# Seven products instead of eight in two more places of a four-layer graph network, with GpSimd taking the element-wise steps around them

## The chip, the cores and the metric

The kernel is one program on one core of a Trainium2 chip. The core has a matrix engine (TensorE, in the profile PE, its weight loads PEld), a vector engine (VectorE, DVE), a scalar engine for activation functions (ScalarE, ACT), a general engine (GpSimd, POOL) and an engine that here only issues transfers (SyncE, SP). Each works through a queue of its own in order, and semaphores tie the queues together. Matmuls read SBUF and write PSUM, which is divided into banks of 128 x 512 float32. The metric is the time of one execution in device microseconds. Before the change three runs took 2252.04, 2249.4 and 2255.14 us (median 2252.04).

## The reference

The input x is (128, 64, 256) in float32: 128 graphs of 64 nodes with 256 features. Four layers follow, each of the form x = x + f(relu(layernorm(x))). Two of them matter here, both in the third layer:

```python
h = relu(einsum('ts,bsh->bth', adj, x @ Wg0 + bg0))
h = relu(einsum('ts,bsh->bth', adj, h @ Wg1 + bg1))
for p in range(1, 5):                       # MAX_SKIP = 4
    nw = Tv // p                            # Tv = 64 nodes
    wins = h[:, :nw * p, :].reshape(Bv * nw, p, Hd)
    last = lstm_last(Wih[p - 1], Whh[p - 1], bih[p - 1], bhh[p - 1], wins)
    h = h.at[:, arange(nw) * p + (p - 1), :].set(last)
```

That is two graph convolutions and then four LSTMs, one for each window length p. The LSTM of a window runs p steps from a zero state with c = sigmoid(f) * c + sigmoid(i) * tanh(g) and h = sigmoid(o) * tanh(c), and its last h replaces the window's last node. With p = 1 a window is one node: one step, no recurrent product, no forget gate, and every one of the 64 nodes is replaced.

## The kernel before

**Layout.** The 8192 rows (128 graphs x 64 nodes) are 16 blocks of 512. X0 to X15 are sixteen SBUF tiles of 128 x 1024 float32, one a block. In the third layer the features are the partitions: `big` is four tiles (groups of four blocks), seen by `nodes` (L1767) as 2 feature halves x 64 nodes x 32 graphs.

**Order.** PE, DVE and ACT instructions go through a recording helper, `Ordered.__getattr__.call` (L788, its call is L799), so in the profile all of them carry L799 and tiles tell them apart. GpSimd instructions carry their own lines. Inside a stage a tile scheduler puts the instructions into each engine's queue; there is no hand-written order in the two stages of the change. A tile that is taken again makes its next writer wait for its readers.

**Third layer, graph convolutions** (`layer2`, L2147; a step is `block`, L2174). For block i: the first weight, `ps<-a,w`, two PSUM tiles of 128 x 512 with two matmuls each, then a maximum with a table N0 on DVE into `g`; `features` of block i-1 (`ps<-BDA,y`, the adjacency product, relu on ACT into `big`); `mixed` of block i+1 (`ps<-BDA,h`, its two halves evacuated into `a`, one by DVE and one by ACT, in turn through `move`, L1487); the second weight, `pt<-w,g`, with the sum into `y` on DVE; and the layer norm of block i+2, whose X tile is then written to DRAM (`xs<-X`, L2156), since the LSTMs use the X tiles as scratch. There are 4 `ps` banks, 2 `pt` banks and 2 `pe` banks.

**LSTMs** (`windows`, L2204; `lstm`, L2294). For each p the nodes are cut into chunks of up to 16 windows of one group; a chunk is 256 columns at p = 1, 16 chunks in all, taken in pairs. `gates` (L2321) forms the pre-activations of one or two gates. A weight of 256 x 256 is split into four 128 x 128 quarters and the operand into four parts of 128 x W columns, and seven products of such quarters and their sums (`product`, L2337, in the order 1, 6, 7, 5, 2, 4, 3) replace eight. The partial sums live in four banks a, b, f and d of a ring of seven `ps` banks. Product 1 is copied to Z (`ls_z`) on ACT, and DVE adds: Z += product 6; U = Z + product 7; one quarter = U + product 5; then Z plus bank f (after product 4) and Z plus bank d (after product 3). ACT applies sigmoid or tanh to the four quarters. The sums of the operand's parts are three DVE subtractions into `ls_tx` (one of 128 x 512, two of 128 x 256), those of the weights four DVE instructions a weight.

At p = 1 the input and cell gates (0, 2) of one chunk go together by seven products. The output gate (3) goes alone: four matmuls of 512 columns into two banks, with two activations. DVE multiplies i and g (`X<-ls_g`, 128 x 1024), ACT takes the tanh, and `last_state` (L2396) multiplies on DVE in two instructions of 128 x 512 into `big`.

**Weights.** `load` (L2224) and `weights` (L2232) place the LSTM weights: those for odd p in X tiles (Whh in X0 to X3, Wih in X4 to X7), those for even p in tiles of their own; the DMAs are on SP (L2239). The weights for p + 1 are asked for after the first pair of p's chunks. X8 to X15 are rings for c, h, U and others.

## Time and profile before

| quantity | value |
|---|---|
| median of three runs | 2252.04 us |
| the profiled execution's own time | 2254.63 us |
| its span | 2252.8 us |
| mean granted clock of TensorE | 0.997 |
| busy: PE, DVE, ACT, POOL | 2214.0, 1610.7, 1143.7, 7.2 us |
| POOL instructions | 33 |
| p = 1: first PE instruction, first of p = 2 | 677.64, 830.53 us |
| PE idle at the start of p = 1 | 0.85 us |
| DVE busy from 500 to 550, 600 to 650 us (of 50) | 43.6, 19.7 us |

The profile is of one execution, and all sums below are made against that execution. A busy share is an average over stages: only some 167 us of third-layer blocks (16 of 10.46 us, PE rows from 593.81 to 604.27) and the 153 us of p = 1 concern the change. In rows of the timeline the first number is the start in us, the second the time from the first start to the last end of the group; the next row's start tells when the engine went on, since the ends of pipelined instructions overlap the next start. A float32 matmul leaves two records, so "x8" in a row of matmuls is four matmuls. "[0.20 <-DMA ...]" behind a row is idle time of the engine before it and what ended it.

### The profile page before, as it was taken

What the parts mean: (1) busy time and instruction counts of PE and PEld (TensorE: products, weight loads), DVE (VectorE), ACT (ScalarE), POOL (GpSimd) and SP (SyncE); (2) the same over time, 40 slices, a digit from 0 to 9 for tenths busy, and PEclk for the clock granted to TensorE, in tenths of its full rate; (3) what the DMA queues carried; (4) which work ended last, traced back from release to release, by engine and by line L of the source; (5) the groups of instructions that cost most, each with busy time, mean ns of one, the idle gap of its engine ahead of it and who ended that gap; (6) DMA issues with size and microseconds to landing.
All of it is one profiled execution on the core that took longest, in us unless ns stands there. A gap on an engine that the chain in (4) does not pass through costs nothing.

```text
span 2252.8 us, 33666 instructions
## 1 busy us (share of the span) xinstructions
PE 2214.0 (98%) x12617; PEld 1614.5 (72%) x12617; DVE 1610.7 (71%) x4073; ACT 1143.7 (51%) x2500; POOL 7.2 (0%) x33
## 2 busy tenths in 40 slices
PE   7999998999999999999999999999999999999999
PEld 4554444667777778888999999888888555555654
DVE  8777576888538776676767676756955787777767
ACT  5667864665435663444444443433634664444431
POOL 1000000000000000000000000000000000000000
PEclk9999999999999999999999999999999999999999
DMA  6000220122000000000100001000001000000001
GB/s 181 1 1 10 75 54 27 59 93 47 1 24 5 1 19 1 1 1 1 38 1 1 1 1 60 16 1 1 13 1 51 29 1 15 15 20 20 15 24 48
DMA packets 61070, 54.88 MB, mean 24 GB/s; under 512 B 15203, under 2 KB 58724, under 8 KB 60900
## 3 DMA queue, kind: packets, MB, share of 16 engines
q1 hardware_dynamic: 60900, 52.66, 7.6%
q8 instruction: 101, 1.65, 0.3%
q14 instruction: 69, 0.57, 0.1%
HBM read 35.86 MB, written 16.78 MB: 23 GB/s over the span
## 4 chain that ended last, share of the span: by engine, by line
PE 77%; DVE 4%; ACT 1%; issue 1%; DMA 0%; ACTq 0%; DVEq 0%
PE ps L799 70%; PE pt L799 4%; PE acc L799 3%; DVE sm_m L799 1%; DVE X L799 1%; PE pe L799 1%; DVE aw L799 1%; DVE XV L799 0%; ACT ls_g L799 0%; ACT h L799 0%; DMA ls_w<-in_L_gnn_Wih_t_dram 0%; DVE lin_s L799 0%; DVE lin_p L799 0%; DVE hT L799 0%; DVE n_st L799 0%
## 5 line engine op out<-in xcount | busy, mean ns | idle before, releaser
L799 ACT ACTIVATE ls_g<-ls_g,ls_b 128x512 f32<-128x512 f32 (+4 forms) x472 | 243.3, 565 | 146.8 <-DVE ls_g L799 144.7
L799 ACT ACTIVATE ls_g<-ps,ls_b 128x256 f32<-128x256 f32 (+3 forms) x268 | 115.6, 470 | 335.9 <-PE ps L799 332.8
L799 PE MATMUL ps<-z,w 128*128 128x512 f32 x512 | 257.1, 624 | 0.0
L799 PE MATMUL ps<-big,X 128*128 128x176 f32 (+3 forms) x848 | 212.7, 366 | 0.1
L799 DVE TENSOR_TENSOR ls_g<-ls_z,ps 128x512 f32<-128x512 f32 (+5 forms) x258 | 147.3, 577 | 90.7 <-PE ps L799 89.0
L799 PE MATMUL ps<-ls_tx,X 128*128 128x160 f32 (+2 forms) x960 | 206.9, 326 | 1.4 <-DVE ls_tx L799 0.9
L799 PE MATMUL ps<-X,X 128*128 128x160 f32 (+1 forms) x896 | 199.1, 306 | 0.0
L799 PE MATMUL ps<-X,ls_w 128*128 128x256 f32 x640 | 190.5, 379 | 0.1
L799 PEld LDWEIGHTS ps<-ls_tx,X 128*128 128x128 f32 x960 | 161.7, 190 | 16.3 <-DVE X L799 4.7
L799 DVE TENSOR_TENSOR aw<-at,ed_OST 128x1024 f32<-128x1024 f32 x128 | 150.3, 1220 | 28.7 <-PE ps L799 28.5
L799 ACT ACTIVATE r<-ps 128x512 f32<-128x512 f32 x256 | 129.4, 621 | 74.6 <-PE ps L799 74.5
L799 PEld LDWEIGHTS ps<-big,X 128*128 128x128 f32 x848 | 145.9, 190 | 29.7 <-issue 19.4
L799 DVE TENSOR_TENSOR X<-ls_g 128x1024 f32<-128x1024 f32 (+2 forms) x108 | 117.5, 1088 | 50.6 <-ACT ls_g L799 50.6
L799 PEld LDWEIGHTS ps<-X,X 128*128 128x128 f32 x896 | 148.4, 190 | 0.0
L799 PE MATMUL ps<-X,ls_s 128*128 128x256 f32 x480 | 142.7, 379 | 0.0
L799 PEld LDWEIGHTS ps<-z,w 128*128 128x128 f32 x512 | 87.5, 191 | 67.6 <-issue 60.4
L799 PE MATMUL ps<-ls_tx,ls_s 128*128 128x256 f32 x464 | 134.7, 379 | 0.0
L799 PEld LDWEIGHTS ps<-X,ls_w 128*128 128x128 f32 x640 | 121.3, 190 | 16.8 <-DVE X L799 0.5
L799 PE MATMUL ps<-ls_tx,ls_w 128*128 128x256 f32 x464 | 133.3, 380 | 0.0
L799 PE MATMUL ps<-big,ls_w 128*128 128x256 f32 x464 | 131.9, 379 | 0.7 <-ACT ls_z L799 0.7
L799 PE MATMUL ps<-aw,ed_ODT 128*32 128x512 f32 x1024 | 122.0, 593 | 0.1
L799 PE MATMUL ps<-ed_S,Q 64*128 64x512 f32 x512 | 121.0, 604 | 0.9 <-DVE X L799 0.9
(560 smaller groups left out, 3938.7 us busy)
## 6 DMA issues: line engine op xcount, KB each, us to landing
X<-in_x_dram SPq DMA_DIRECT2D x32, 512.0 KB
xs<-X SPq DMA_DIRECT2D x16, 512.0 KB
X<-xs SPq DMA_DIRECT2D x16, 512.0 KB
out_dram<-X SPq DMA_DIRECT2D x31, 256.0 KB
X<-in_L_gnn_Wih_t_dram SPq DMA_DIRECT2D x4, 512.0 KB
ls_w<-in_L_gnn_Wih_t_dram SPq DMA_DIRECT2D x4, 512.0 KB
ls_w<-in_L_gnn_Whh_t_dram SPq DMA_DIRECT2D x4, 512.0 KB
w<-in_L_gnn_W_t_dram SPq DMA_DIRECT2D x2, 512.0 KB
```

The costliest lines, as they stand in the source:

```text
L799: i = method(*a, **kw)
```

## The change

Three things change, in two stages.

- Graph convolution, blocks 5 to 15 (`SEVEN = 5`): the first weight goes by seven products of 128 x 128 x 256 columns. The sums of W0's quarters are formed once (`sums0`, four DVE instructions of 128 x 128, into X2); the sums of the operand `a` are three GpSimd subtractions for each block into X0 or X1 (one of 128 x 512, two of 128 x 256); both halves of `a` are evacuated by ACT. Z is an ACT copy into X3, and DVE makes five additions and three maxima (256, 256 and 512 columns). Products 1, 6, 7 and 5 are issued before `features`, products 2, 4 and 3 after it.
- p = 1 (`single`): a pair of chunks goes together. A is the gates i and g of the first chunk, B those of the second, O the output gates of both; each is seven products with two matmuls of 256 columns. GpSimd multiplies i and g (one instruction of 128 x 1024 for each chunk), and `last_state` of both chunks is four GpSimd instructions of 128 x 512.
- The X tiles are allocated in pairs, and at p = 1 the gates stand in a ring `g_` of five pairs of X tiles (X8/X9, X10/X11, X12/X13, X0/X1, X2/X3) instead of the `ls_g` tiles. So the Whh weights of p = 3, which go into X0 to X3, can be loaded only when GpSimd has read the last of these tiles. In the queues of the changed kernel SP's two Whh loads wait for GpSimd, and the four DVE sums of that weight stand in DVE's queue in p = 2, the first of them ahead of the U addition of the second call of `gates`; the first two sums of p = 3's Wih stand ahead of an addition of p = 1's last O gate and ahead of the first Z addition of p = 2.

```diff
 MAX_SWEEPS = 480
+SEVEN = 5
...
 class Ops:
...
         nc.sync.dma_start(self.AT[:], io["adj_t"])
-        self.X = []
-        for i in range(NB):
-            self.X.append(self.c(f"X{i}", P, TPB, D))
+        self.X2 = [self.c(f"X{i}", P, 2, TPB, D) for i in range(0, NB, 2)]
+        self.X = [x[:, i] for x in self.X2 for i in range(2)]
         self.load_x(0)
...
     def load_x(self, i):
...
         W0, W1, b1, N0 = self.tables2
-        hs, as_, ys = {}, {}, {}
+        hs, as_, ts, ys = {}, {}, {}, {}
...
             if i < NB:
...
                 a = as_[i] = pool.tile([P, 2, BT], F32, name="a")
-                self.mix(psum, hs.pop(i), self.BDA, lambda dc, p: self.move(a[:, dc, :], p[:]))
+                seven = i >= SEVEN
+                self.mix(psum, hs.pop(i), self.BDA,
+                         lambda dc, p: (self.act_copy if seven else self.move)(a[:, dc, :], p[:]))
+                if seven:
+                    T = ts[i] = spare(i % 2, 4, 256)
+                    B = a[:].rearrange("p k (h w) -> p k h w", h=2)
+                    sub = lambda out, x, y: nc.gpsimd.tensor_tensor(out, x, y, op=ALU.subtract)
+                    sub(T[:, 0:2], B[:, :, 1], B[:, 0])
+                    sub(T[:, 2], B[:, 1, 1], T[:, 0])
+                    sub(T[:, 3], B[:, 1, 0], T[:, 2])
+        def eight(i, a, g):
+            for hc in range(2):
+                p = psum.tile([P, BT], F32, name="ps")
+                for kc in range(2):
+                    self.mm(p[:], W0[:, kc, hc * P:(hc + 1) * P], a[:, kc, :], kc == 0, kc == 1)
+                o.tt(g[:, hc, :].rearrange("p (b n) -> p b n", n=N), p[:].rearrange("p (b n) -> p b n", n=N),
+                     N0[:, hc, None, :].to_broadcast([P, BT // N, N]), ALU.max)
+            return lambda: None
+        def seven(i, a, g):
+            T, B = ts.pop(i), a[:].rearrange("p k (h w) -> p k h w", h=2)
+            b = {1: B[:, 0, 0], 2: B[:, 1, 0], 3: B[:, 1, 1], 5: T[:, 0], 7: T[:, 1], 6: T[:, 2], 4: T[:, 3]}
+            V = g[:].rearrange("p k (h w) -> p k h w", h=2)
+            banks = {}
+            def product(m, bank, first):
+                if first:
+                    banks[bank] = (psum.tile([P, BT], F32, name="ps") if bank in "af" else ps0.tile([P, BT], F32, name="pe"))
+                p = banks[bank][:, 0:256]
+                nc.tensor.matmul(p, self.S0[m], b[m], start=first, stop=True, skip_group_check=True)
+                return p
+            def bound(hc, out, p):
+                by = lambda x: x.rearrange("p (b n) -> p b n", n=N)
+                o.tt(by(out), by(p), N0[:, hc, None, :].to_broadcast([P, by(p).shape[1], N]), ALU.max)
+            Z, U = spare(3, 4, 256)[:, i % 4], V[:, 1, 1]
+            self.act(Z, product(1, "a", True), AF.Copy)
+            o.add(Z, Z, product(6, "b", True))
+            o.add(U, Z, product(7, "f", True))
+            o.add(V[:, 1, 1], U, product(5, "d", True))
+            def rest():
+                bound(0, V[:, 0, 0], product(2, "a", False))
+                o.add(V[:, 1, 0], Z, product(4, "f", False))
+                o.add(V[:, 0, 1], Z, product(3, "d", False))
+                bound(0, V[:, 0, 1], V[:, 0, 1])
+                bound(1, g[:, 1, :], g[:, 1, :])
+            return rest
+        def sums0():
+            A = [[W0[:, kc, hc * P:(hc + 1) * P] for kc in range(2)] for hc in range(2)]
+            S1, S2, S3, S4 = (spare(2, 8, P)[:, x] for x in range(4))
+            o.add(S1, A[1][0], A[1][1])
+            o.sub(S2, S1, A[0][0])
+            o.sub(S4, A[0][1], S2)
+            o.sub(S3, A[0][0], A[1][0])
+            self.S0 = {1: A[0][0], 2: A[0][1], 3: S4, 4: A[1][1], 5: S1, 6: S2, 7: S3}
+        def spare(k, n, m):
+            return self.X[k][:].rearrange("p t d -> p (t d)").rearrange("p (n m) -> p n m", m=m)
...
             v = self.nodes(i // 4)
...
                     nc.hold()
+            if i == SEVEN - 1:
+                sums0()
             a = as_.pop(i)
             g = pool.tile([P, 2, BT], F32, name="g")
-            for hc in range(2):
-                p = psum.tile([P, BT], F32, name="ps")
-                for kc in range(2):
-                    self.mm(p[:], W0[:, kc, hc * P:(hc + 1) * P], a[:, kc, :], kc == 0, kc == 1)
-                o.tt(g[:, hc, :].rearrange("p (b n) -> p b n", n=N), p[:].rearrange("p (b n) -> p b n", n=N),
-                     N0[:, hc, None, :].to_broadcast([P, BT // N, N]), ALU.max)
+            rest = (seven if i >= SEVEN else eight)(i, a, g)
             if i:
                 features(i - 1)
+            rest()
             mixed(i + 1)
...
             for jj in range(0, TPB, 2):
...
             o.add(bias[:], bias[:], bh[:])
-            flat = [x[:].rearrange("p t d -> p (t d)") for x in self.X]
+            flat = [x.rearrange("p t d -> p (t d)") for x in self.X]
+            self.g_ = Ring([self.X2[i][:].rearrange("p x t d -> p x (t d)") for i in (4, 5, 6, 0, 1)])
             self.c_, self.h_, self.th_ = Ring(flat[12:15]), Ring(flat[8:10]), Ring(flat[10:12])
...
             self.lp = gp, tp, zp, psum, bias
...
                     o.sub(S3, A[0][0], A[1][0])
-                    out.append({1: A[0][0], 2: A[0][1], 3: S4, 4: A[1][1], 5: S1, 6: S2, 7: S3,
-                                "A": A})
+                    out.append({1: A[0][0], 2: A[0][1], 3: S4, 4: A[1][1], 5: S1, 6: S2, 7: S3})
                 return out
...
             ready = weights(1)
...
                     two[-1]["last"] = p == 4 and n + 2 >= len(chunks)
+                    if p == 1:
+                        self.single(two, Ws[0])
+                        continue
                     for t in range(p):
...
                             self.lstm(p, t, ch, Ws)
...
             G = gp.tile([P, 2, 1024], F32, name="ls_g")
-            if p == 1 and len(xs) == 1:
-                for k in range(2):
-                    ps = psum.tile([P, BT], F32, name="ps")
-                    for kc in range(2):
-                        self.mm(ps[:, 0:2 * W].rearrange("p (w b) -> p w b", b=32), Ws[0]["A"][k][kc][:, xs[0], :],
-                                node(kc), kc == 0, kc == 1)
-                    self.act(G[:, 0, 2 * W * k:2 * W * (k + 1)].rearrange("p (h w b) -> p h w b", h=2, b=16),
-                             ps[:, 0:2 * W].rearrange("p (w h b) -> p h w b", h=2, b=16), fs[0],
-                             bias=bias[:, p - 1, 2 * xs[0] + k:2 * xs[0] + k + 1])
-                return G
             n = len(xs)
...
             banks = {}
...
-    def last_state(self, H, at, W, *factors):
+    def single(self, two, A):
+        nc, o = self.nc, self.o
+        gp, tp, zp, psum, bias = self.lp
+        I, F, G, O = range(4)
+        data = []
+        for ch in two:
+            H, at = self.nodes(ch["q"]), slice(ch["w0"], ch["w1"])
+            T = tp.tile([P, 4, 256], F32, name="ls_tx")[:].rearrange("p n (w b) -> p n w b", b=16)
+            o.sub(T[:, 0:2], H[:, :, at, 16:32], H[:, 0, at, :].rearrange("p w (h b) -> p h w b", h=2))
+            o.sub(T[:, 2], H[:, 1, at, 16:32], T[:, 0])
+            o.sub(T[:, 3], H[:, 1, at, 0:16], T[:, 2])
+            data.append({1: H[:, 0, at, 0:16], 2: H[:, 1, at, 0:16], 3: H[:, 1, at, 16:32],
+                         5: T[:, 0], 7: T[:, 1], 6: T[:, 2], 4: T[:, 3]})
+        def gates(pairs, act):
+            tile = self.g_.next()
+            V = tile.rearrange("p x (k h w) -> p x k h w", k=2, h=2)
+            banks = {}
+            def product(m, bank, first):
+                if first:
+                    banks[bank] = psum.tile([P, 2, 256], F32, name="ps")
+                for i, (x, b) in enumerate(pairs):
+                    nc.tensor.matmul(banks[bank][:, i, :].rearrange("p (w b) -> p w b", b=16), A[m][:, x, :], b[m],
+                                     start=first and i == 0, stop=i == 1, skip_group_check=True)
+                return banks[bank][:]
+            Z = zp.tile([P, 2, 256], F32, name="ls_z")[:]
+            U = self.u_.next().rearrange("p (x w) -> p x w", x=2)
+            a = product(1, "a", True)
+            self.act(Z, a, AF.Copy)
+            o.add(Z, Z, product(6, "b", True))
+            o.add(U, Z, product(7, "f", True))
+            o.add(V[:, :, 1, 1], U, product(5, "d", True))
+            a = product(2, "a", False)
+            act(V[:, :, 0, 0], a, 0)
+            o.add(V[:, :, 1, 0], Z, product(4, "f", False))
+            act(V[:, :, 1], V[:, :, 1], 1)
+            o.add(V[:, :, 0, 1], Z, product(3, "d", False))
+            act(V[:, :, 0, 1], V[:, :, 0, 1], 0)
+            return tile
+        def apart(out, a, k):
+            for i, (x, f) in enumerate(((I, AF.Sigmoid), (G, AF.Tanh))):
+                self.act(out[:, i], a[:, i], f, bias=bias[:, 0, 2 * x + k:2 * x + k + 1])
+        def together(out, a, k):
+            self.act(out, a, AF.Sigmoid, bias=bias[:, 0, 2 * O + k:2 * O + k + 1])
+        cells = []
+        for b in data:
+            V = gates(((I, b), (G, b)), apart)
+            nc.gpsimd.tensor_tensor(V[:, 0], V[:, 0], V[:, 1], op=ALU.mult)
+            self.act(V[:, 1], V[:, 0], AF.Tanh)
+            cells.append(V)
+        V = gates([(O, b) for b in data], together)
+        for i, ch in enumerate(two):
+            self.last_state(self.nodes(ch["q"]), slice(ch["w0"], ch["w1"]), 256, V[:, i], cells[i][:, 1], engine=nc.gpsimd)
+    def last_state(self, H, at, W, *factors, engine=None):
...
             y = H[:, k, at, :].rearrange("p w (h b) -> p h w b", h=2)
-            self.o.mul(y, *(x[:, 2 * W * k:2 * W * (k + 1)].rearrange("p (h w b) -> p h w b", h=2, b=16) for x in factors))
+            (engine or self.nc.vector).tensor_tensor(y, *(x[:, 2 * W * k:2 * W * (k + 1)].rearrange("p (h w b) -> p h w b", h=2, b=16) for x in factors), op=ALU.mult)
```

## The prediction, made before the changed kernel was run

> **What bounds the kernel now.** I read the page first: PE is busy for 98% of the span and holds most of the chain of work that ended last. Only PE time that goes, and PE waits that come, move the end.
>
> ```profile
> span 2252.8 us, 33666 instructions
> PE 2214.0 (98%) x12617; PEld 1614.5 (72%) x12617; DVE 1610.7 (71%) x4073; ACT 1143.7 (51%) x2500; POOL 7.2 (0%) x33
> ...
> PE 77%; DVE 4%; ACT 1%; issue 1%; DMA 0%; ACTq 0%; DVEq 0%
> ```
>
> Then the timeline of PE over one block of the graph convolution, and over one chunk of p = 1. Both are gapless, at a clock of 1.00.
>
> ```profile
> 593.81 3.60 PE L799 MATMUL ps<-a,w 128*128 128x512 f32 x8
> 597.24 1.95 PE L799 MATMUL ps<-BDA,y 128*128 128x128 f32 x16
> 599.03 1.95 PE L799 MATMUL ps<-BDA,h 128*128 128x128 f32 x16
> 600.82 3.62 PE L799 MATMUL pt<-w,g 128*128 128x256 f32 x16
> ```
>
> ```profile
> 746.11 2.75 PE L799 MATMUL ps<-ls_tx,X 128*128 128x256 f32 x12
> 748.70 1.89 PE L799 MATMUL ps<-big,X 128*128 128x256 f32 x6
> 750.42 1.03 PE L799 MATMUL ps<-ls_tx,X 128*128 128x256 f32 x4
> 751.28 4.46 PE L799 MATMUL ps<-big,X 128*128 128x256 f32 x14
> 755.58 0.59 PE L799 MATMUL ps<-ls_tx,X 128*128 128x256 f32 x2
> ```
>
> From start to start, a 512-column record takes 3.43 / 8 = 0.43 us and a 256-column one 0.86 / 4 = 0.2155 (row 750.42). The chunk is 28 short and 8 long records, 9.47 us. The long ones, the output gate, lie between the seven products: they give DVE and ACT time to catch up. Next, DVE in the same chunk, POOL's few instructions, and what DVE did beside one of them.
>
> ```profile
> 747.24 0.69 DVE L799 TENSOR_TENSOR ls_z<-ls_z,ps 128x512 f32<-128x512 f32 x1 [0.55 <-PE ps L799]
> ...
> 752.09 0.69 DVE L799 TENSOR_TENSOR ls_tx<-big 128x512 f32<-128x512 f32 x1
> ...
> 753.28 0.88 DVE L799 TENSOR_TENSOR ls_tx<-big,ls_tx 128x256 f32<-128x256 f32 x2
> ```
>
> ```profile
> L1808 POOL TENSOR_TENSOR big<-big 128x512 f32<-128x512 f32 x1 | 1.3, 1263 | 0.1
> ...
> L1811 POOL TENSOR_TENSOR ed_key<-ed_key,ed_less 128x4 f32<-128x4 f32 x1 | 0.2, 203 | 0.1
> ```
>
> ```profile
> 41.77 1.26 POOL L1808 TENSOR_TENSOR big<-big 128x512 f32<-128x512 f32 x1
> ```
>
> ```profile
> 38.09 0.21 DVE L799 SCALAR_TENSOR_TENSOR f_x<-f_OA,f_NB,f_x 64x2 f32<-64x2 f32 x1
> ...
> 41.98 1.06 DVE L799 SCALAR_TENSOR_TENSOR f_h_t<-f_h_r,f_x,f_h_s 64x1 f32<-64x1 f32 x1
> ```
>
> The two POOL rows give (1263 - 203) / 508 = 2.09 ns an element: 128x256 0.73 us, 128x1024 2.33 us. The DVE instruction at 41.98 has one element a partition and all operands in SBUF; its kind took 0.21 at 38.09, and here it ended at 43.04, with POOL's multiplication at 43.03. I read that as DVE held until POOL was done.
>
> **The change, part by part.** Graph convolution: the product with W0 was 8 x 0.43 = 3.43 us and becomes 14 x 0.2155 = 3.02; 11 blocks gain 4.6 us. What comes in its place:
>
> - Three POOL subtractions a block, 1.26 + 0.73 + 0.73. They start when ACT has evacuated the second half of `a`, 0.85 us (0.2 + 0.60) after `ps<-BDA,h` ends. Product 6 needs the second of them, ready at 0.85 + 1.26 + 0.08 + 0.73 = 2.9, and begins after `pt` and product 1, at 3.45 + 0.43 = 3.9: hidden by 1.0. The third is for product 4, later still. Without that cover, or if DVE holds POOL, up to 1 us a block; I take 0.
> - Five additions and three maxima on DVE, about 0.43 each and 0.69 for the 512 one, for two of 0.69 and the COPY of `a`. DVE was busy 19.7 of 50 us there: covered. Behind product 3 stand an addition and the 512 maximum before `pt` may start, 0.2 + 0.4 + 0.7 = 1.3 us; the 1.79 us of `ps<-BDA,h` cover it. In block 15 there is no next `mixed`: 1.3 us on the path.
> - `sums0`, four DVE instructions of 128x128, under 0.3 each: in DVE's idle time; without it 1 us once.
>
> p = 1: a pair was 2 x 9.47 = 18.94 us and is 84 x 0.2155 = 18.10; 8 pairs gain 6.7 us. What comes in its place:
>
> - The chain in a gate. Product 1 ends at 0.86. If ACT is free Z is copied by 1.66 (0.2 + 0.60), added by 2.6, U by 3.5 (product 7 ends at 2.59), and product 4, which reuses U's bank, starts at 4.31. In a gate that follows another, ACT first has the previous gate's last quarter (0.2 + 0.69 + 0.85): U at 3.65, slack 0.65. No loss alone.
> - The 128x1024 multiplication on POOL, 2.33 where DVE had 1.23 (row of `X<-ls_g`, 745.46). ACT's tanh waits for it, with the next gate's two activations of product 2 behind it. Multiplication from 1.85 to 4.2, tanh to 5.25; those activations begin 0.7 us later than their product allows and are done before product 4's quarter is added at 6.1. Hidden, by 0.2 at least.
> - `last_state`, four POOL multiplications a pair. The nearest row is L1808, 1.26; on DVE the same strided output cost nothing extra (1.29 for two). They run from 1.15 to 6.5 us after the O gate's end, and POOL is wanted for the next multiplication at 7.9: margin 1.4, or 0.35 an instruction. DVE's queue in that stretch holds the next pair's `ls_tx` subtractions, two SBUF operands each, the last of them between the Z and U additions. One subtraction held for 0 to 1.26 us, less the slack: 0 to 0.6; two of them, up to 1.9. I take 0.5 a pair, seven times: 3.5 us, ends 0 and 13.
> - The first pair. Both chunks' subtractions precede it, one more of 0.60 ahead of what product 6 needs; PE already waited 0.85 there: 0.6 us.
>
> The step that is moved: Whh of p = 3. Its two DMAs leave the graph convolution (SP at 500.13 and 503.05) and wait on SP for POOL's last multiplication of p = 1, 6.5 us after PE's last product; nothing else is due on SP before p = 3. The nearest price of two such loads:
>
> ```profile
> 829.87 1.19 SPq L2239 DMA_DIRECT2D X<-in_L_gnn_Wih_t_dram  x2
> ```
>
> ```profile
> 835.26 0.69 DVE L799 TENSOR_TENSOR X<-X,X 128x512 f32<-128x512 f32 x1 [0.20 <-DMA X<-in_L_gnn_Wih_t_dram]
> ```
>
> 5.4 us from issue. So Whh is there 11.9 us after p = 1's end, its first sum on DVE takes 0.69, and the U addition of the second call behind it ends at 13.3. Product 4 of that call is due at 6.03 + 2.15 = 8.2: PE waits 5.1 us. Wih's sum ahead of the first Z addition waits too, about 1 us, which is part of the 5.1. Ends: 2 (no hold, loads faster) and 8 (POOL a third dearer).
>
> Sum: -4.6 - 6.7 + 1.3 + 3.5 + 0.6 + 5.1 = -0.8 us. Against the profiled execution (2254.63, which is 2.6 above the median) that is 2253.8; against the median 2252.04, 2251.2.
>
> On the hold there is a rule. The Trainium skill, "SBUF — State Buffer", section "Who interferes with whom", says that DVE and GpSimd share a pair of ports, that a DVE instruction with two SBUF inputs contends with a GpSimd one that reads SBUF, and that the loser blocks fully; by it the `ls_tx` subtractions are exposed and the additions from PSUM are not, as the 1.06 us row has it, and the sum stands as above, while with no hold it would be 3.5 us lower. It speaks against this change. "GPSIMD Engine Reference", section "Engine selection", puts element-wise work on VectorE, about twice as slow on GpSimd; the rows here say 1.26 against 0.65.
>
> **The rivals.**
>
> 1. *No hold that matters, faster.* The 41.98 row is one case. If subtractions fall between POOL's instructions, 3.5 goes to 0 and the transition falls to 2 to 4: -4.6 - 6.7 + 1.3 + 0.6 + 2 = -7.4, 2244.6. For it: DVE's subtractions have free places before the O gate ends. Against: the last ones are behind the V additions in order.
> 2. *Held twice a pair, slower.* Two subtractions held on each boundary, 1.9 x 7 = 13.3 for 3.5: 2261. It decides where a second one falls under a `last_state`.
> 3. *POOL becomes the bound of p = 1, slower.* If `last_state` takes over 1.6 us with its strided output, POOL's next multiplication is late, tanh with it, and ACT's queue with the Z copy behind it. At 2.0 us: 4 x 0.74 - 1.4 = 1.6 a pair, 13 us, and 3 at the transition: 2267.
> 4. *The change does not do what it says:* if a 256-column matmul cost over 0.246 us, seven products would gain nothing; rows of the same form say 0.2155, so I give it nothing.
>
> **How the numbers follow.** A measurement here tells about 0.3%, 6.8 us, from no change. Forecast 0.40 (own range 2246 to 2258), rival 1 0.24, rival 2 0.20, rival 3 0.16. Faster by over 0.3% (below 2245.3): 0.20 of rival 1 and 0.05 of the forecast, where the term of the transition or of the holds falls to its lower end: 0.25. Slower (above 2258.8): 0.16 of rival 2, all of rival 3 and 0.02 of the forecast: 0.34. Same: the rest, 0.41. The range leaves out 0.1 below (rival 1 with a cheaper tail of block 15) and 0.1 above (rival 3 beyond 2.0 us, or with rival 2): 2243 to 2267.
>
> **What would show it.** POOL with 81 multiplications and subtractions more, `last_state` near 1.26; block starts 10.05 us apart from block 5 on; pairs at 18.1 plus a wait of `ps<-ls_tx,X` for DVE; `ls_tx` rows over 1 us beside POOL rows; one PE wait of some 5 us early in p = 2 behind the Whh loads. I am wrong if `last_state` is over 1.6 us, if no `ls_tx` row is long, or if blocks stay at 10.46.

## The result, and the profile after

The changed kernel takes 2261.14 us (median of six runs, 2260.57 to 2265.86) against 2252.5 for the kernel before (six runs, 2249.4 to 2255.14). The ratio is 1.0045 with a 95% interval of 1.0035 to 1.0055: about 10 us slower, 8 to 12 (the two medians are 8.6 us apart). Forecast was 0.8 us faster.

The page of the changed kernel (span; busy time, share and instructions of each engine; then the chain that ended last):

```profile
span 2261.6 us, 34224 instructions
PE 2207.4 (98%) x12779; PEld 1643.0 (73%) x12779; DVE 1632.7 (72%) x4124; ACT 1155.0 (51%) x2522; POOL 121.4 (5%) x114
...
PE 75%; DVE 6%; issue 1%; ACT 1%; DMA 0%; ACTq 0%; DVEq 0%; SPq 0%
```

PE is busy 6.6 us less, yet the span is 8.8 us longer, and DVE's share of the chain went from 4% to 6%: PE waits for DVE. The starts of the stages, read from PE's timeline, say where. "Convolution" runs from `ps<-BDA,y` of block 4 to the first matmul of p = 1, "p = 1" to the first matmul with `ls_w`, "p = 2" to the first of 160 columns. ("Block 4" is the step of block 4, the last one before the change sets in. The stretch ahead of it, whose code is the same, takes 550.4 to 555.7 us in the profiles of this document, so the span of one profile is not the measure. Where the code of a stage is the same, the convolution and p = 1 repeat within some 0.4 us; the rest lies between 1155.5 and 1156.9.)

| profile | convolution | p = 1 | p = 2 | rest |
|---|---|---|---|---|
| before | 122.24 | 152.89 | 266.50 | 1155.77 |
| after | 118.66 | 159.96 | 273.82 | 1156.30 |
| after minus before | -3.6 | +7.1 | +7.3 | +0.5 |
| the prediction's terms | -3.3 | -2.6 | +5.1 | 0 |

The convolution did what was foreseen. PE's timeline of the changed kernel, the starts of two blocks, and its only wait there, in block 15:

```profile
600.08 0.59 PE L800 MATMUL ps<-a,w 128*128 128x256 f32 x2
...
610.13 0.59 PE L800 MATMUL ps<-a,w 128*128 128x256 f32 x2
...
666.46 3.29 PE L800 MATMUL pt<-w,g 128*128 128x256 f32 x14 [0.68 <-DVE g L800]
```

Blocks are 10.05 us apart, for 10.46 before. POOL's groups (operation, shapes, count, busy time, mean ns, idle time ahead):

```profile
L2518 POOL TENSOR_TENSOR big<-X,X 128x512 f32<-128x512 f32 x32 | 45.6, 1454 | 23.7 <-ACT X L800 23.7
L2507 POOL TENSOR_TENSOR X<-X 128x1024 f32<-128x1024 f32 x16 | 37.7, 2358 | 71.6 <-ACT X L800 71.6
L2167 POOL TENSOR_TENSOR X<-a,X 128x256 f32<-128x256 f32 x22 | 16.8, 764 | 1.7
L2167 POOL TENSOR_TENSOR X<-a 128x512 f32<-128x512 f32 x11 | 13.9, 1267 | 263.3 <-ACT a L800 263.3
```

All prices but one are within 5% of those estimated (0.73, 1.26, 2.33); `last_state` takes 1.454 for 1.263. Now one pair of p = 1. PE's timeline, then DVE's, then POOL's:

```profile
777.87 1.13 PE L800 MATMUL ps<-ls_tx,X 128*128 128x256 f32 x4 [1.06 <-DVE X L800]
...
795.50 1.03 PE L800 MATMUL ps<-big,X 128*128 128x256 f32 x4
797.59 1.13 PE L800 MATMUL ps<-ls_tx,X 128*128 128x256 f32 x4 [1.06 <-DVE X L800]
```

```profile
794.15 1.38 DVE L800 TENSOR_TENSOR ls_tx<-big,ls_tx 128x256 f32<-128x256 f32 x1
795.45 0.68 DVE L800 TENSOR_TENSOR ls_z<-ls_z,ps 128x512 f32<-128x512 f32 x1
796.04 0.89 DVE L800 TENSOR_TENSOR ls_tx<-big,ls_tx 128x256 f32<-128x256 f32 x1
796.86 0.67 DVE L800 TENSOR_TENSOR X<-ls_z,ps 128x512 f32<-128x512 f32 x1
```

```profile
793.56 5.73 POOL L2518 TENSOR_TENSOR big<-X,X 128x512 f32<-128x512 f32 x4 [2.90 <-ACT X L800]
```

A pair takes 797.59 - 777.87 = 19.72 us where its 84 records need 18.10. Two subtractions of 0.42 us stand at 1.38 and 0.89, both inside POOL's four multiplications; behind the second waits the U addition (796.86), and behind that PE's product 4, due at 795.50 + 0.86 = 796.36 and begun at 797.59, 1.23 us late. The additions between, with one operand in PSUM, have their 0.6 to 0.7 us. POOL is slowed in its turn: 5.73 / 4 = 1.43.

At the start of p = 2 the same happens with more instructions in line. DVE, POOL, PE, and the table by stretches (busy time of each engine, then the granted clock, DMA share, GB/s):

```profile
833.66 2.91 DVE L800 TENSOR_TENSOR ls_tx<-big,ls_tx 128x256 f32<-128x256 f32 x2
836.49 1.75 DVE L800 TENSOR_TENSOR X<-X 128x512 f32<-128x512 f32 x1
```

```profile
833.53 5.83 POOL L2518 TENSOR_TENSOR big<-X,X 128x512 f32<-128x512 f32 x4 [3.45 <-ACT X L800]
```

```profile
840.30 2.07 PE L800 MATMUL ps<-ls_tx,ls_w 128*128 128x256 f32 x4 [3.31 <-DVE X L800]
```

```profile
836.00:840.00 4.00, 0.99 (x5) 0.53 (x3) 4.00 (x5) 0.84 (x2) 3.36 (x3) 0.89 0.31 85
840.00:842.00 2.00, 1.70 (x4) 1.44 (x5) 1.44 (x3) 0.00 (x0) 0.00 (x0) 0.50 0.59 172
842.00:844.00 2.00, 2.00 (x6) 1.55 (x6) 1.29 (x2) 0.74 (x2) 0.00 (x0) 0.50 0.48 190
844.00:846.00 2.00, 2.00 (x7) 1.56 (x6) 0.80 (x2) 1.17 (x3) 0.00 (x0) 0.51 0.00 0
```

Two subtractions and a sum of Wih, 0.76 + 0.69 us of work, took 4.6 us under POOL's last four multiplications; PE waited 3.31 us, and from 840 to 846 its granted clock was 0.50 (0.89 as the mean of 836 to 840 puts the beginning near 839.1). The Whh loads, on which the prediction put 5.1 us, were issued at 837.72, and the sum that uses them (846.23 on DVE) shows no wait for them.

### The profile page after: what moved, and what is told of

Read it like the earlier page. It is cut to its first block, busy times and chain, and to the rows that moved or that the text cites. A ratio compares the mean times of both kernels' runs of the same rounds, so it can differ in the third digit from the quotient of the medians.

```text
span 2261.6 us, 34224 instructions
## 1 busy us (share of the span) xinstructions
PE 2207.4 (98%) x12779; PEld 1643.0 (73%) x12779; DVE 1632.7 (72%) x4124; ACT 1155.0 (51%) x2522; POOL 121.4 (5%) x114
## 4 chain that ended last, share of the span: by engine, by line
PE 75%; DVE 6%; issue 1%; ACT 1%; DMA 0%; ACTq 0%; DVEq 0%; SPq 0%
PE ps L800 67%; PE pt L800 4%; PE acc L800 3%; DVE X L800 2%; PE pe L800 1%; DVE sm_m L800 1%; DVE ls_tx L800 1%; DVE aw L800 1%; DVE XV L800 0%; ACT ls_g L800 0%; DVE ls_z L800 0%; ACT h L800 0%; ACT big L800 0%; DVE lin_s L800 0%; DVE lin_p L800 0%
## 5 line engine op out<-in xcount | busy, mean ns | idle before, releaser
L800 ACT ACTIVATE ls_g<-ls_g,ls_b 128x512 f32<-128x512 f32 (+5 forms) x408 | 208.1, 559 | 124.7 <-DVE ls_g L800 122.7
L800 PE MATMUL ps<-ls_tx,X 128*128 128x256 f32 (+2 forms) x1088 | 238.8, 334 | 11.0 <-DVE X L800 9.4
L800 ACT ACTIVATE ls_g<-ps,ls_b 128x256 f32<-128x256 f32 (+2 forms) x204 | 80.5, 438 | 305.4 <-PE ps L800 304.3
L800 PE MATMUL ps<-X,X 128*128 128x160 f32 (+2 forms) x918 | 205.6, 308 | 0.0
L800 PEld LDWEIGHTS ps<-ls_tx,X 128*128 128x128 f32 x1088 | 184.2, 190 | 28.6 <-DVE X L800 16.9
L800 DVE TENSOR_TENSOR ls_g<-ls_z,ps 128x512 f32<-128x512 f32 (+3 forms) x226 | 125.6, 561 | 78.8 <-PE ps L800 77.2
L800 PE MATMUL ps<-big,X 128*128 128x256 f32 (+2 forms) x816 | 181.2, 332 | 0.1
L800 PEld LDWEIGHTS ps<-big,X 128*128 128x128 f32 x816 | 139.4, 190 | 8.8 <-DVE ls_g L800 0.4
L800 DVE TENSOR_TENSOR X<-ls_z,ps 128x512 f32<-128x512 f32 (+4 forms) x185 | 112.6, 609 | 37.6 <-PE ps L800 34.7
L800 DVE TENSOR_TENSOR X<-ls_g 128x1024 f32<-128x1024 f32 (+2 forms) x92 | 97.9, 1064 | 38.9 <-ACT ls_g L800 38.8
```

The source lines that it names most:

```text
L800: i = method(*a, **kw)
```

## The experiments

Theories: **H**, DVE instructions with two SBUF operands are held by POOL, and that is the loss of p = 1 and at the start of p = 2. **S**, three seven-product gates in a row leave the chain Z, U, product 4 too little time, whoever multiplies. **L**, Whh's late load costs the start of p = 2. **C**, the halved clock there is a consequence of PE's wait. The expectation of e1 names its first stage by block 5; it is block 4's first matmul to which its times belong.

| run | convolution | p = 1 | p = 2 | ratio to before (95%) |
|---|---|---|---|---|
| e1, convolution only | 118.86 | 153.15 | 266.35 | 0.9991 (0.9981 to 1.0001) |
| e2, multiplications on DVE | 118.67 | 159.37 | 270.74 | 1.0021 (1.0012 to 1.0031) |
| e3, subtractions on POOL too | 118.67 | 174.13 | 270.17 | 1.0097 (1.0078 to 1.0116) |
| e4, `last_state` on DVE | 118.67 | 161.79 | 269.04 | 1.0041 (1.0026 to 1.0055) |
| e5, subtractions from PSUM | 118.96 | 149.84 | 271.03 | 0.9987 (0.9976 to 0.9998) |
| e6, Whh loaded early | 119.02 | 160.23 | 273.76 | 1.0042 (1.0026 to 1.0059) |
| e7, PE busy in the wait | 118.66 | 159.95 | 276.75 | 1.0056 (1.0035 to 1.0076) |
| e8, product 1 ahead | 118.66 | 154.94 | 273.41 | 1.0019 (1.0010 to 1.0029) |
| e9, last pair as before | 118.66 | 161.88 | 266.80 | 1.0031 (1.0016 to 1.0045) |
| e10, subtractions placed | 118.90 | 159.16 | 271.54 | 1.0037 (1.0024 to 1.0050) |
| e11, placed, both ends as before | 118.90 | 151.90 | 267.18 | 0.9986 (0.9977 to 0.9995) |

Each row's stages are those of one profile, and some hold a stretch in which the granted clock was 0.50: 6.8 us in p = 1 of e2, twice 6.8 us in p = 1 of e3, twice 3.4 us in p = 1 of e10, and in p = 2 6.8 us in the changed kernel and e6 and 3.4 us in e7 and e8. In e2 and e10 PE's queue has also shifted: twelve and eight records of p = 1's last gate stand behind p = 2's first matmul, so 2.6 and 1.7 us of p = 1 are counted under p = 2. e7 has two runs, e6 three, e3 and e9 four.

### e1: the convolution's part alone

```diff
-                    if p == 1:
-                        self.single(two, Ws[0])
-                        continue
...
+            if p == 1 and len(xs) == 1:
+                for k in range(2):
...
```

The lines that come back are those of the kernel before, the output gate by four matmuls.

> The changed kernel with p = 1 as before (output gate by four matmuls, multiplications on DVE); only the graph convolution's first weight goes by seven products. In the profiles of before and after, the stretch from block 5's first matmul to p = 1's first took 125.7 and 122.1 us, p = 1 152.9 and 160.0, p = 2 266.5 and 273.8. All theories: blocks 10.05 us apart, that stretch 122.1. Theory H (DVE instructions with two SBUF operands are held by POOL, and this makes the loss in p = 1 and at the start of p = 2): with no POOL work in p = 1 that stage is 152.9 again and p = 2 266.5, total about 3.6 us below before, 2249. Theory L (the loss at the start of p = 2 is that of weights loaded late): Whh of p = 3 still waits for blocks that use X0 to X3, but has all of p = 1 to land, so p = 2 is 266.5 as well. Rival: the convolution's part costs time that its own stretch does not show, total 2252 or more.

p = 1 and p = 2 are back at the times of before, and the convolution keeps its gain. So the whole loss lies in p = 1's part of the change. Of the total, 3.6 us are at the edge of what a comparison here can tell: the interval just reaches 1.

### e2: i*g and last_state on DVE

```diff
-            nc.gpsimd.tensor_tensor(V[:, 0], V[:, 0], V[:, 1], op=ALU.mult)
+            o.mul(V[:, 0], V[:, 0], V[:, 1])
...
-            self.last_state(self.nodes(ch["q"]), slice(ch["w0"], ch["w1"]), 256, V[:, i], cells[i][:, 1], engine=nc.gpsimd)
+            self.last_state(self.nodes(ch["q"]), slice(ch["w0"], ch["w1"]), 256, V[:, i], cells[i][:, 1])
```

> The changed kernel with p = 1's multiplications (i*g and last_state) on DVE instead of POOL; products, tiles and loads as in the changed kernel. Theory H: no long ls_tx row is left, no PE wait behind a held subtraction; DVE has 6 subtractions, 15 additions, 2 + 4 multiplications a pair, about 2.6 + 9.2 + 2.4 + 2.4 = 16.6 of 18.1 us, so it just keeps up: p = 1 145 to 152 us, p = 2 266.5 to 269, total about 2244 (2241 to 2251). Theory S (three seven-product gates in a row are too tight for the chain Z, U, product 4, whoever multiplies): p = 1 stays at 157 to 162, total about 2259. Theory L: p = 2 still loses, since Whh still waits for the last multiplication of p = 1: 270 to 274.

Against H as it was put: no subtraction is held (the longest of 128x256 takes 0.42 us), yet p = 1 gains nothing; with the shifted records it takes 162.0 us, 3 of them by the halved clock. DVE has another queue. DVE's timeline in e2, then PE's:

```profile
695.53 2.62 DVE L800 TENSOR_TENSOR big<-X,X 128x512 f32<-128x512 f32 x4
698.07 1.42 DVE L800 TENSOR_TENSOR ls_tx<-big,ls_tx 128x256 f32<-128x256 f32 x4
```

```profile
698.63 6.72 PE L800 MATMUL ps<-ls_tx,X 128*128 128x256 f32 x16 [2.99 <-DVE ls_tx L800]
```

At the first boundary between pairs the four multiplications stand ahead of four subtractions that PE needs at once: a wait of 2.99 us, with the halved clock behind it. From 776.86 to 796.61 a later pair takes 19.75 us, with DVE busy for 16.9 of them; PE's waits there are 0.54 us for U, whose Z addition stands behind the multiplication i*g (793.94, 1.23 us), and 0.34 us for `ls_tx`. Theory S foresaw the size, but this run cannot tell S from a DVE queue with too much in it. p = 2 is 4.2 us longer than before: 2.6 us are the shifted records, most of the rest PE waits of 0.95 and 0.34 us for DVE. Theory L had forecast a loss of that size here for another reason; e6 decides on L.

### e3: the subtractions on POOL too

```diff
+        sub = lambda out, x, y: nc.gpsimd.tensor_tensor(out, x, y, op=ALU.subtract)
...
-            T = tp.tile([P, 4, 256], F32, name="ls_tx")[:].rearrange("p n (w b) -> p n w b", b=16)
-            o.sub(T[:, 0:2], H[:, :, at, 16:32], H[:, 0, at, :].rearrange("p w (h b) -> p h w b", h=2))
+            T = both[:, k].rearrange("p (n w b) -> p n w b", n=4, b=16)
+            sub(T[:, 0:2], H[:, :, at, 16:32], H[:, 0, at, :].rearrange("p w (h b) -> p h w b", h=2))
...
```

`both` is an `ls_g` tile, free at p = 1; the other two subtractions change likewise.

> The changed kernel with the six subtractions of a pair (ls_tx) on POOL as well, into tiles two pairs deep so that they run ahead. POOL's work in p = 1 grows from 10.4 to about 16 us of a pair's 18.1; DVE keeps no instruction with two SBUF operands there except the sums of weights. Theory H: the waits of 1.06 us a pair for DVE go, p = 1 falls to 145 to 150 us although POOL has half as much work again; the start of p = 2 loses 2 us or less; total 2243 to 2249. Theory S, and a theory that POOL's slowness is what costs (tanh late behind it, ACT's queue behind tanh): p = 1 stays at 158 or grows, total 2260 or more.

H alone would have made it fast; it is the slowest. Part of that is an accident of order: the `ls_tx` tiles are free now, so p = 2's subtractions moved ahead in DVE's queue, and the first waits for POOL's writes into `big`, with a U addition behind it (PE waits 6.62 us, and 6.54 once more, and after each the clock is halved for 6.8 us). DVE's timeline in e3:

```profile
704.32 0.69 DVE L800 TENSOR_TENSOR ls_tx<-big 128x512 f32<-128x512 f32 x1 [5.64 <-POOL big L2520]
```

Later pairs are free of it and still take 19.6 us, now behind ACT. ACT's timeline in e3:

```profile
780.40 1.06 ACT L800 ACTIVATE X<-X 128x1024 f32<-128x1024 f32 x1 [3.23 <-POOL X L2509]
781.37 0.82 ACT L800 ACTIVATE X<-ps,ls_b 128x256 f32<-128x256 f32 x2
782.08 2.12 ACT L800 ACTIVATE X<-X,ls_b 128x512 f32<-128x512 f32 x4
784.10 0.58 ACT L800 ACTIVATE ls_z<-ps 128x512 f32<-128x512 f32 x1
```

tanh stood 3.23 us for POOL's i*g, and four activations and the next gate's Z copy stood behind it. This is rival 3 of the prediction, reached by more POOL work instead of a dearer `last_state`. POOL's four multiplications into `big` took 4.96 us here (from 773.10), 1.24 each against 1.263 for L1808 in the profile of before: the strided output cost nothing here, with no DVE instruction of two SBUF operands beside them.

### e4: last_state alone on DVE

```diff
-            self.last_state(self.nodes(ch["q"]), slice(ch["w0"], ch["w1"]), 256, V[:, i], cells[i][:, 1], engine=nc.gpsimd)
+            self.last_state(self.nodes(ch["q"]), slice(ch["w0"], ch["w1"]), 256, V[:, i], cells[i][:, 1])
```

> The changed kernel with last_state alone on DVE; POOL keeps i*g (two of 2.36 us a pair). Theory H: the subtractions of the next pair fall where POOL is idle; the waits of 1.06 us go; the two multiplications may hold a last_state on DVE now and then: p = 1 146 to 152, total 2243 to 2251. Theory S: p = 1 157 to 162, total about 2259. If it is the multiplication i*g that matters and not last_state, the 1.06 us waits stay.

p = 1 takes 161.79, against H's 146 to 152. The 1.06 us waits went, as by H, and three smaller ones came, 0.26 for `ls_tx`, 0.39 for Z and 0.38 for U in each pair (PE's timeline): 19.94 us a pair. The first is DVE's queue as in e2, `last_state` ahead of the next pair's subtractions. The other two are ACT's line in the O gate: tanh waits 1.08 us for POOL's i*g (at 786.54), four activations and the Z copy stand behind it, and DVE idles 3.10 us until that copy is done (790.13).

### e5: the hold by itself

The three runs above changed the load of an engine along with the hold. This one leaves every instruction on its engine and takes one operand of the subtractions from PSUM. It leaves out the right value of that operand, so it is a measurement of time and no version to use. The order is nearly the same; at a pair's boundary two of the subtractions stand one place later on DVE, the last of them behind U, and the Z copy stands one activation earlier on ACT.

```diff
-            o.sub(T[:, 0:2], H[:, :, at, 16:32], H[:, 0, at, :].rearrange("p w (h b) -> p h w b", h=2))
-            o.sub(T[:, 2], H[:, 1, at, 16:32], T[:, 0])
-            o.sub(T[:, 3], H[:, 1, at, 0:16], T[:, 2])
+            R = self.still.rearrange("p (n w b) -> p n w b", n=2, b=16)
+            o.sub(T[:, 0:2], H[:, :, at, 16:32], R)
+            o.sub(T[:, 2], T[:, 0], R[:, 0])
+            o.sub(T[:, 3], T[:, 2], R[:, 1])
```

`still` is a PSUM bank, written once before.

> The changed kernel, but at p = 1 the second operand of the six ls_tx subtractions is read from a PSUM bank that holds a constant (so the recurrent sums have wrong values); number, sizes and places of all instructions as in the changed kernel, POOL's work too. Theory H (a DVE instruction with two SBUF operands is held by POOL): ls_tx rows are 0.42 and 0.69 us at most, the wait of 1.06 us for DVE at the fourth product of every pair's first gate goes, a pair takes 18.4 to 18.7 us instead of 19.72, p = 1 about 150 to 152. Theory S (no hold matters, the chain of three seven-product gates in a row is too tight): pairs stay at 19.5 or more, p = 1 158 to 160. The start of p = 2, whose subtractions and sums of weights are unchanged, still loses 5 us or more by H.

p = 1 falls by 10.1 us, to 149.84, as H says. DVE's timeline of e5, and POOL's `last_state` beside it:

```profile
766.62 0.41 DVE L800 TENSOR_TENSOR ls_tx<-ls_tx,pt 128x256 f32<-128x256 f32 x1
766.96 0.68 DVE L800 TENSOR_TENSOR X<-ls_z,ps 128x512 f32<-128x512 f32 x1
767.55 0.41 DVE L800 TENSOR_TENSOR ls_tx<-ls_tx,pt 128x256 f32<-128x256 f32 x1
```

```profile
765.53 4.98 POOL L2523 TENSOR_TENSOR big<-X,X 128x512 f32<-128x512 f32 x4 [2.90 <-ACT X L800]
```

A pair takes 18.38 us (763.16 to 781.54 in PE's timeline of e5) and has no wait left that the profile marks. The 19.5 or more of S did not come, and 1.34 of the 1.62 us that a pair lost went with the hold. The rows of the changed kernel give the same without e5's shifted places: the two subtractions took 0.96 and 0.47 us too long, and without these 1.43 us U, which ended at 797.53, would have been done 0.26 us before product 4 was due; product 4 began 1.23 us late, and its four records took 0.11 us longer than 0.86. The 0.28 us that are left lie in delays of 0.03 and 0.24 us at product 4 of the other two gates. The start of p = 2 keeps its 3.31 us wait, since its subtractions and sums are unchanged, but the clock stays at 1.00, and p = 2 takes 271.03, 4.5 us above before where 5 or more were expected.

### e6: Whh loaded early

```diff
-            self.g_ = Ring([self.X2[i][:].rearrange("p x t d -> p x (t d)") for i in (4, 5, 6, 0, 1)])
+            self.g_ = Ring([self.X2[i][:].rearrange("p x t d -> p x (t d)") for i in (4, 5, 6)])
...
-            tile = self.g_.next()
+            tile = self.g_.next() if act is apart else gp.tile([P, 2, 1024], F32, name="ls_g")[:]
```

> The changed kernel with p = 1's gate tiles in a ring of three X pairs and the two ls_g tiles, so that X0 to X3 are free and Whh of p = 3 is loaded and summed before p = 1. Theory L (the late load of Whh costs the start of p = 2, 5.1 us in the prediction): p = 2 falls from 273.8 to 267 to 269. Theory H: the load was not waited for; the last multiplications of p = 1 on POOL still hold DVE's subtractions and Wih sums, p = 2 stays at 272 to 274. p = 1 itself 159 to 161 by both.

p = 2 takes 273.76, as in the changed kernel: L is out as the cause of what was measured.

### e7: PE kept busy in the wait

```diff
             a = product(2, "a", False)
+            if p == 2 and not t and not self.warmed:
+                self.warmed = True
...
+                for _ in range(15):
+                    self.mm(q[:, 0:P], self.ident[:], self.ones[:])
...
```

> The changed kernel with 15 matmuls of 128 columns (0.22 us each, 3.3 in all, result unused) put into PE's queue where it waits 3.3 us at the start of p = 2. In the changed kernel's profile the granted clock is 0.50 from 840 to 846 us, after that wait, and matmuls of 256 columns take 0.43 us a record there. Theory C (the clock is halved because PE stood idle for 3.3 us, and that costs 2.9 us more): with PE busy the clock stays at 1.00 and p = 2 takes 270.5 to 271.5 instead of 273.8, although PE has 3.3 us more work. Rival (the matmuls are slow for another reason, such as transfers or POOL at that time): p = 2 273.5 to 274.5.

The clock did stay at 1.00, but p = 2 took 276.75, 2.9 us more. A stretch of e7 after the wait (columns as above), and DVE's timeline:

```profile
842.00:844.00 2.00, 2.00 (x14) 1.59 (x13) 2.00 (x4) 0.00 (x0) 0.15 (x1) 1.00 0.81 238
```

```profile
846.78 0.69 DVE L800 TENSOR_TENSOR X<-X 128x512 f32<-128x512 f32 x1 [1.35 <-DMA X<-in_L_gnn_Whh_t_dram]
```

DVE comes to the Whh sums earlier, 11.2 us after p = 2's first matmul for 14.75 in the changed kernel, and now does wait for the load, 1.35 us; PE waits 1.64 and 1.73 us in two places soon after, and the clock falls to 0.63 later (852 to 856). So the halved clock did follow from PE's idle time, as C says. Its price cannot be read from e7, in which the load is next in line behind the wait that hid it. It can be read from e5: there p = 2 has the same waits, 0.79 and 3.31 us, at a clock of 1.00, and takes 2.8 us less than in the changed kernel.

### e8: product 1 of the next gate ahead

```diff
             self.act(Z, a, AF.Copy)
+            self.rest()
             o.add(Z, Z, product(6, "b", True))
...
```

`rest` is products 2, 4 and 3 of the gate before, and what follows them.

> The changed kernel with product 1 of the next gate, and its copy to Z, issued ahead of products 2, 4 and 3 of the gate before, through all of p = 1; the same products, tiles and POOL instructions. Each chain Z, U, product 4 gains one product (0.86 us) of slack. Theory S+H (the waits come from chains in order with less slack than a held subtraction and ACT's queue take): most of the 1.6 us a pair goes, pairs 18.2 to 18.9, p = 1 147 to 152, start of p = 2 still held; total 2250 to 2256. If the limit is an engine's rate rather than latency (DVE or POOL short of time in a pair), pairs stay at 19.5 or more, total 2260.

Pairs take 19.20 us (PE's waits at 713.35, 732.55, 751.75), half a microsecond less than 19.72, p = 1 5.0 us less. That misses its expectation (18.2 to 18.9, p = 1 147 to 152), and the 19.5 or more of its rival did not come either. The waits are now 0.8 us for Z on ACT, so more slack helps, and ACT's line is what is left.

### e9: the last pair as before

```diff
-                    if p == 1:
+                    if p == 1 and n + 2 < len(chunks):
                         self.single(two, Ws[0])
```

> The changed kernel, with the last of the eight pairs of p = 1 computed as before (output gates by four matmuls, multiplications on DVE), the other seven as changed. Theory H for the start of p = 2 (its subtractions and Wih sums on DVE were held by POOL's last four multiplications, PE waited 0.8 and 3.3 us, and its clock was halved for 6 us after that): with POOL idle by then p = 2 takes 266 to 268 us instead of 273.8, and its granted clock stays at 1.00. Rival (p = 2's start suffers from the order of the instructions or from the loads that now come late, whoever multiplies): p = 2 270 us or more. p = 1: seven pairs of 19.72 and one of about 19, 158 to 160. Total 2252 to 2255.

p = 2 takes 266.80, within 0.3 us of before, with the clock at 1.00: the loss at its start is POOL's last work. In e9 DVE does wait there for p = 3's Wih, 0.45 us, and it costs nothing. Not all of it is gained: p = 1 takes 161.88, 1.9 us more than in the changed kernel and above the 158 to 160 expected. 0.84 us of that are the last pair's own products (18.94 for 18.10), 0.78 are two PE waits in it (0.54 and 0.24); DVE waits there 1.27 us for the Whh load (824.31). The total, 2258.42, is above the 2252 to 2255 expected.

### e10 and e11: the subtractions where POOL is idle

```diff
-        for b in data:
+        for k, b in enumerate(data):
             V = gates(((I, b), (G, b)), apart)
+            early(k)
...
```

`early` issues the three subtractions of chunk k of the next pair, and holds DVE's order there.

> The changed kernel with the next pair's six subtractions moved on DVE: three behind the last addition of gate A, three behind that of gate B (into X0 to X3, a pair ahead), where in the changed kernel's profile DVE sits idle for 1.75 and 2.0 us and POOL has not begun its multiplication. The O gates stand in the ls_g tiles. The same instructions on every engine. Theory H: none of the subtractions is held, the wait of 1.06 us goes, a pair takes 18.3 to 18.8, as with the operand from PSUM (18.38); p = 1 149 to 152. Rival (a pair takes 19.7 because DVE is short of time in all): 19.5 or more. The start of p = 2 is as in the changed kernel, 271 to 274. Total 2249 to 2254.

> As the kernel with moved subtractions, with the first and the last pair of p = 1 computed as before, so that POOL works in the six middle pairs only and is idle when the weights of p = 2 are summed and when p = 2 starts. Theory H: p = 1 about 6 x 18.4 + 2 x 18.95 + 1 to 3 = 149.5 to 152, p = 2 266.3 to 268, the convolution 3.6 us shorter: total 2246 to 2250, 0.1 to 0.3% below the kernel before. Rival: if pairs stay at 19.7 or p = 2 at 270 or more, total 2255 or more.

In both the undisturbed pairs take about 18.46 us (746.01 to 764.48 in PE's timeline of e11). DVE's and POOL's timelines of e11:

```profile
752.07 0.68 DVE L800 TENSOR_TENSOR X<-big 128x512 f32<-128x512 f32 x1
752.78 0.89 DVE L800 TENSOR_TENSOR X<-big,X 128x256 f32<-128x256 f32 x2
```

```profile
746.48 4.99 POOL L2548 TENSOR_TENSOR big<-ls_g,X 128x512 f32<-128x512 f32 x4 [2.78 <-ACT ls_g L800]
753.47 2.43 POOL L2537 TENSOR_TENSOR X<-X 128x1024 f32<-128x1024 f32 x1 [2.00 <-ACT X L800]
```

The subtractions lie in POOL's pause, to within 0.2 us, and POOL's multiplications into `big` are back at 1.25 us. e10 as a whole misses its expectation: p = 1 is 159.16 for 149 to 152, with the shifted records 160.9. PE waits 2.11 and 2.27 us where sums of p = 2's weights, two SBUF operands each, are held by POOL in the first two pairs (one of 0.69 us takes 2.84 at 689.21), and 3.11 us in the third, where a subtraction of p = 2 waits 3.81 us for POOL's writes into `big`, as in e3; the clock is halved for 3.4 us after the first and the third. e11, in which POOL rests in the first and the last pair, has p = 1 at 151.90 and p = 2 at 267.18, both as expected. At 2247.73 us against 2251.21 it is the one complete version whose interval lies below the kernel before, if by 0.14% only. Nearly all of that is the convolution's part: p = 1 and p = 2 together take 419.1 us in e11, 419.4 before and 419.5 in e1.

## Why the prediction was wrong

**The convolution** was right: 3.3 us forecast, 3.6 measured, with PE's wait in block 15 at 0.68 us for 1.3. POOL's subtractions were hidden, as costed.

**The products of p = 1** were right: 84 records at 0.2155 in the pair. **The first pair** was put at 0.6 us for its own subtractions; that wait stayed at 0.86. What came was another: a sum of p = 2's weights, held by POOL's first multiplication, with the U addition of gate B behind it. DVE's timeline of the changed kernel:

```profile
681.36 2.72 DVE L800 TENSOR_TENSOR ls_s<-ls_s,ls_w 128x512 f32<-128x512 f32 x1
```

It cost PE 1.90 us at 685.93. The prediction had looked at DVE's queue for the subtractions alone.

**The term that failed most** is "I take 0.5 a pair, seven times: 3.5 us". The hold was the right mechanism and its signs came: long `ls_tx` rows, pairs of 18.1 us plus a wait for DVE, `last_state` under 1.6 us. Its size was wrong: 1.34 us at each boundary instead of 0.5, and 10.1 us in p = 1 by e5. The prediction had the right case in its list, two subtractions held, "up to 1.9", and chose a value near that of one. Every boundary of the changed kernel has the two (0.96 and 0.47 us in the rows shown), with the second between the Z and U additions. The slack that was to be taken off was smaller as well. The forecast has "U at 3.65, slack 0.65" in a gate that follows another. ACT's timeline of the changed kernel, for the O gate that began at 785.78 and for the next pair's first gate, which began at 792.05:

```profile
786.04 2.13 ACT L800 ACTIVATE X<-X,ls_b 128x512 f32<-128x512 f32 x4
788.07 0.58 ACT L800 ACTIVATE ls_z<-ps 128x512 f32<-128x512 f32 x1
...
792.28 1.76 ACT L800 ACTIVATE X<-X,ls_b 128x1024 f32<-128x1024 f32 x2
793.95 0.57 ACT L800 ACTIVATE ls_z<-ps 128x512 f32<-128x512 f32 x1
```

The forecast let two activations of the previous gate stand ahead of the Z copy, which puts it 1.74 us into the gate. In the O gate four stand there and Z is copied 2.3 us in; U ended at 790.16, and product 4 was due at 790.09. That is part of the 0.28 us a pair for which the prediction said "No loss alone". In the first gate, where the hold falls, Z is copied 1.9 us in, and the slack without the hold would have been 0.26 us.

Rival 2, two held on each boundary, came out nearest, 2261 for 2261.14, partly by luck: it has 1.9 a boundary for 1.34, and nothing for the weights' sum in the first pair, for the 0.28 a pair or for the clock.

The Trainium skill, "SBUF — State Buffer", section "Who interferes with whom", which the prediction weighed, agrees with e5: with one operand in PSUM the subtraction stays at 0.42 us, with two in SBUF it reaches 1.38.

**The transition**: "PE waits 5.1 us" for Whh was near in size, 7.3, and wrong in cause. The loads were in time because DVE was late by itself: 4.6 us for 1.45 us of work, by the hold (e9 without POOL's last work: 266.80; e6 with an early load: 273.76). The halved clock, not foreseen, is in the 7.3: fourteen records of 256 columns after 840.30 took 5.9 us for 3.0. e7 shows that the Whh load is a real second wait behind the first: it landed 12.5 us after p = 2's first matmul, where the prediction had 11.9 after the end of p = 1. So the load's time was right, and what failed is the step that has DVE ready for it before then.

**The range** of 2243 to 2267 held the measured time; the forecast was on the wrong side, and its own range, 2246 to 2258, did not hold it. The 6.7 us of products were saved on PE, and p = 1 lost 13.8 us elsewhere: seven boundaries of 1.34, eight times 0.28, and some 2.1 us for the weights' sum in the first pair.

## What to carry to other kernels

When matmuls are saved in a stage in which PE is busy all the time, ask first what the other engines did in the time that goes: with the output gate's four matmuls (e1) PE has one wait in p = 1, and without them moving the multiplications to DVE (e2), to POOL (the change) or more to POOL (e3) all lost. Work given to GpSimd has to be set against every DVE instruction with two SBUF operands in the same stretch, sums of weights and prefetches among them. Placing those in GpSimd's pauses (e11) took the loss away, but p = 1 and p = 2 together gained only 0.3 us on before, no more than the noise; a gain from the products of p = 1 was not shown in any complete version. And a wait that hides another is no proof that the other is free (e7).

## What the runs showed of the hardware

- The hold goes both ways: DVE's 128x256 subtraction rose from 0.42 to as much as 1.38 us in p = 1, and POOL's 128x512 multiplication from 1.24 (e3) to 1.43 (the changed kernel).
- In these profiles the granted clock changes only on a grid. In each of them the times of its changes are whole multiples of 3.41 us apart, with the grid lying differently in each: 839.15 and 845.98 in the changed kernel; 694.38, 697.79, 731.92 and 735.34 in e10. The length of a wait alone does not decide whether the clock is halved: 3.31 us did it in the changed kernel, 2.99 in e2 and 2.11 in e10, while 3.31 in e5 and 2.95 in e3 (687.66) did not. What separates the two kinds here is PE's idle time inside one step of that grid. Steps of the changed kernel, of e10 (two) and of e5 (two; columns as above, PE's busy time first):

```profile
835.74:839.15 3.41, 1.25 (x6) 0.76 (x4) 3.41 (x4) 0.84 (x2) 3.41 (x3) 1.00 0.17 30
```

```profile
701.20:704.62 3.42, 1.56 (x8) 1.02 (x6) 3.42 (x3) 1.30 (x3) 2.63 (x2) 1.00 0.00 0
728.51:731.92 3.41, 1.39 (x5) 0.94 (x6) 2.90 (x6) 1.58 (x4) 2.18 (x1) 1.00 0.00 0
```

```profile
822.76:826.18 3.42, 1.93 (x9) 1.34 (x8) 3.42 (x4) 0.84 (x2) 3.42 (x3) 1.00 0.00 0
826.18:829.59 3.41, 1.59 (x7) 1.43 (x8) 3.39 (x6) 0.00 (x0) 0.88 (x1) 1.00 0.66 195
```

  PE was idle for 2.16 us of the first step and for 2.02 of e10's second, and the clock was 0.50 from the next step on. It was idle for 1.86 us in e10's first step and for 1.49 and 1.82 in e5's two, over which the wait of 3.31 us was spread, and the clock stayed at 1.00. In the third layer of all thirteen profiles every step at full clock with 2.02 us or more of idle time was followed by the halved clock, and none with 1.86 or less was; where between the two the limit lies is not shown. So the 2.9 us that the halved clock cost at the start of p = 2 hang on where the wait falls on the grid. The Trainium skill, "TensorE: Matmul & The Clock Gate", section "HAM oscillation — how this bites in real kernels", gives the rule that PE should have no idle gap over some 3.4 us; the runs here differ from it in that waits of 2.11 and 2.99 us halved the clock too.
